# First chunk of a two-layer kernel: its first two row tiles one at a time instead of as a pair, and twelve identity matmuls at the start instead of eight

## The chip, the cores and the metric

The kernel runs on one core of one Trainium2 chip. The metric is the device time of one execution in microseconds (us), and the time of a kernel is the median of its runs. Five engines work side by side, each with its own instruction queue: PE (TensorE, matrix multiplication and transposes), DVE (VectorE), ACT (ScalarE), POOL (GpSimd) and SP (SyncE, which here only issues DMAs). They meet at semaphores. Every tensor is float32.

## The reference, cut to what matters

The whole is two layers on x of shape (16, 256, 256), that is 4096 rows of 256. Each layer is a LayerNorm, a mixer, a gate and a residual sum. The change sits at the very start of layer 0:

```python
x = L0_attn_x                                   # (16, 256, 256)
xn = _layernorm(x, axis=-1)
s = _L0_attn_ref(xn, ...)                       # diagonal recurrence over 256 steps
h = gelu(einsum('lne,he->lnh', xn, proj1) + proj1_bias)     # 256 -> 1024
g = _silu(einsum('lnh,eh->lne', h, proj2) + proj2_bias)     # 1024 -> 256
x = x + s * g
...                                             # layer 1: attention of 16 heads, a routed low-rank gate
return x
```

## The kernel before, in words

The 4096 rows are cut into 8 chunks (`NCH`) of 512 rows (`CH`). A chunk lies in SBUF as 4 row tiles (`TPC`) of 128 rows, rows on the partitions. For the projection the rows have to be turned, so that the 256 features lie on the partitions: `xnT` holds two feature halves (c = 0, 1) of 128 partitions with 512 columns, one column for each row of the chunk.

Layer 0 goes over the chunks one after the other, layer 1 after it over the same chunks in units of four heads. The first chunk of layer 0 has a function of its own, `start()`, in which nothing is ready yet: the rows, the weights and the identity matrix all have to arrive or be made first. Its helpers are:

- `warm()`: `NWARM` matmuls of the 128x128 identity with itself into a PSUM tile that nobody reads. Each shows as two records in the profile, as every float32 matmul here does.
- `stats(js)`: for each row tile j, bn_stats and bn_aggr on DVE. After an odd tile, DVE adds epsilon to the variances of the two last tiles (`ve`), and POOL raises them to the power of minus one half (`rs`).
- `apply(js)`: DVE subtracts the mean and multiplies by `rs`, which gives `xn`.
- `turn(js)`: PE transposes the two feature halves of each named tile into one PSUM tile `tp`. `keep(js, ps)`: DVE copies that to `xnT` in SBUF.
- `hide(js, f0, f1)`: for blocks fc of 128 hidden features, two matmuls (c = 0, 1) of a block of `p1T` with the columns of `xnT` of the named tiles, into a PSUM tile `ph`; then ACT computes Gelu into `hT[fc]`. There are 8 blocks (`NFC`).

`warm`, `tp` and `ph` tiles come from one ring of four PSUM banks (`ps_mm`, names r1, r2, r3, x), so that a new tile waits until the reader of the tile four places before is done.

Order: PE, DVE, ACT and POOL are wrapped in `InOrder`, which keeps the instructions of each engine in the order in which the code writes them. In between stands `later`, a list of small DVE operations (with a few on ACT and POOL) that make the recurrence's parameters; `later.write(n)` writes the next n of them into the queues, and `later.write("exp")` those up to a mark. They are needed much later, but whoever is behind them on DVE waits for them.

The loads are issued on the queues of SP and ACT at the very start: the four row tiles of chunk 0 one by one on SP, the first two quarters of `p1T` (blocks fc 0 to 1, and 2 to 3) on ACT's queue, then on SP the other half of `p1T`, chunk 1, `p2T` and the rest. None of these waits for a compute engine.

After `start()` come the second projection of chunk 0 (`pf`), the projection of chunk 1, and so on.

Of the kernel before, what the change touches and what calls it, by code (L numbers as in the profile page):

```python
# [11 lines left out]
F32 = mybir.dt.float32  # L12
# [6 lines left out]
P = 128  # L19
# [14 lines left out]
RMS_EPS = 1.1920928955078125e-07  # L34
LORA_SCALE = 32.0 / 16.0
BIG = 1e30
NWARM = 8
MAGIC = 12582912.0


# [1 line left out]
def tile_two_layers(ctx: ExitStack, tc: tile.TileContext, d: dict, out: bass.AP):  # L42
# [386 lines left out]
    with ExitStack() as l0:  # L429
# [22 lines left out]
        ps_mm = Ring("r1", "r2", "r3", "x")  # L452
# [40 lines left out]
        def norm0(ch, between=None):  # L493
            xn = a2.tile([P, TPC, D], F32, tag="xn", name=f"xn0_{ch}")
            layer_norm(sm, X[ch], xn, f"0_{ch}", v0, g0, between)
            return xn

        def turn0(ch, xn):
            xnT = a2.tile([P, 2, CH], F32, tag="xnT", name=f"xnT0_{ch}")
            if ch == 1:  # L500
                transpose_rows(ps_mm, "mm", xn, xnT, f"0_{ch}", a0, v0)
            else:
                transpose_rows(ps_mm, "mm", xn, xnT, f"0_{ch}")
            return xnT


        v0 = ve
        later = Later()
# [27 lines left out]
        def tiny(name, n=1):  # L536
            return w0.tile([P, n], F32, tag=name, name=name)
# [44 lines left out]
        f = tiny("f")  # L582
# [24 lines left out]
        for k in range(8):  # L607
            n = 1 << k
# [485 lines left out]
        def start():  # L1094

            xn = a2.tile([P, TPC, D], F32, tag="xn", name="xn0_0")
            xnT = a2.tile([P, 2, CH], F32, tag="xnT", name="xnT0_0")
            st = sm.tile([P, TPC, 6], F32, tag="ln_st", name="st_0_0")
            mv = sm.tile([P, TPC, 2], F32, tag="ln_mv", name="mv_0_0")
            ve = sm.tile([P, TPC], F32, tag="ln_ve", name="ve_0_0")  # L1100
            rs = sm.tile([P, TPC], F32, tag="ln_rs", name="rs_0_0")
            hT = [hpool.tile([P, CH], F32, tag="hT", name=f"hT_0_{fc}") for fc in range(NFC)]
            X0 = X[0]

            def warm():

                ps = ps_mm.tile([P, CH], F32, tag="mm", name="warm")
                for z in range(NWARM):
                    pe.matmul(ps[:, 0:P], ident, ident, start=True, stop=True)

            def stats(js):
                for j in js:
                    v0.bn_stats(st[:, j, :], X0[:, j, :])
                    v0.bn_aggr(mv[:, j, :], st[:, j, :])
                if js[-1] % 2:
                    z = slice(js[-1] - 1, js[-1] + 1)
                    v0.tensor_scalar(ve[:, z], mv[:, z, 1], LN_EPS, None, ALU.add)
                    g0.tensor_tensor(rs[:, z], ve[:, z], mhalf[:, z], ALU.pow)

            def apply(js):  # L1120
                for j in js:
                    v0.tensor_scalar(
                        xn[:, j, :], X0[:, j, :], mv[:, j, 0:1], rs[:, j : j + 1],
                        ALU.subtract, ALU.mult,
                    )

            def turn(js):
                ps = ps_mm.tile([P, 2, 2 * P], F32, tag="mm", name=f"tp_0_0_{js[0]}")
                for c in range(2):
                    for j2, j in enumerate(js):  # L1130
                        pe.transpose(
                            ps[:, c, j2 * P : (j2 + 1) * P], xn[:, j, c * P : (c + 1) * P], ident
                        )
                return ps

            def keep(js, ps):
                v0.tensor_copy(xnT[:, :, js[0] * P : (js[1] + 1) * P], ps)

            def hide(js, f0, f1):
                z = slice(js[0] * P, (js[1] + 1) * P)  # L1140
                for fc in range(f0, f1):
                    ph = ps_mm.tile([P, 2 * P], F32, tag="mm", name=f"ph_0_{fc}_{js[0]}")
                    for c in range(2):
                        pe.matmul(
                            ph, p1T[:, c, fc * P : (fc + 1) * P], xnT[:, c, z],
                            start=(c == 0), stop=(c == 1),
                        )
                    a0.activation(hT[fc][:, z], ph, AF.Gelu, bias=b1[:, fc : fc + 1])

            warm()  # L1150
            stats((0, 1))
            later.write(4)
            apply((0, 1))
            ps = turn((0, 1))
            stats((2,))
            keep((0, 1), ps)
            stats((3,))
            later.write(3)
            apply((2, 3))
            hide((0, 1), 0, 4)  # L1160
            ps = turn((2, 3))
            later.write("exp")
            keep((2, 3), ps)
            hide((0, 1), 4, NFC)
            hide((2, 3), 0, NFC)
            xn2 = norm0(1, lambda: later.write("angle"))
            later.write("gain")
            xnT2 = turn0(1, xn2)
            later.write()
            return xn, xnT, hT, xn2, xnT2  # L1170

        xn, xnT, hT, xn2, xnT2 = start()
        spread_rope(wraw, g0)

# [18 lines left out]
        xnT = turn0(2, xn3)  # L1193
# [13 lines left out]
        xnT = turn0(3, xn)  # L1207
# [10 lines left out]
        for ch in range(FIRST, NCH - 1):  # L1218
            xn, xnT, norm2, o = middle(ch, xn, xnT, norm2, fill, o)
# [383 lines left out]
    for i in range(LAST):  # L1603
# [4 lines left out]
        n = (i + 3) // 2 if odd else (i + 2) // 2  # L1608
        n = n if n < len(groups) else None
# [69 lines left out]
        if last is not None:  # L1679
            j = FINISH.index(r)  # L1680
# [96 lines left out]
```

## Time and profile before

| what | value |
|---|---|
| time, median of 3 runs | 930.92 us (929.54, 931.18, 930.92) |
| profiled execution, its own time | 930.62 us |
| profiled execution, span from first to last instruction | 928.7 us |
| mean granted TensorE clock over the span | 0.995 |
| PE busy | 908.6 us, 98% of the span |
| DVE, ACT, POOL busy | 71%, 49%, 60% |

A span is shorter than the time of its execution, here by 1.9 us, which lie outside the program's own instructions. "PEclk" or "granted clock" is the share of full speed that the chip's throttle gave TensorE in a stretch. A busy PE is not a PE at its peak, since matmuls overlap and their ends are modelled; the spacing of matmuls of one shape is the better measure of speed. A chain of waits is the list of what released what, followed back from the last instruction.

### The profile page before, as it was taken

What the parts mean: (1) busy time and instruction counts of PE and PEld (TensorE: products, weight loads), DVE (VectorE), ACT (ScalarE), POOL (GpSimd) and SP (SyncE); (2) the same over time, 40 slices, a digit from 0 to 9 for tenths busy, and PEclk for the clock granted to TensorE, in tenths of its full rate; (3) what the DMA queues carried; (4) which work ended last, traced back from release to release, by engine and by line L of the source; (5) the groups of instructions that cost most, each with busy time, mean ns of one, the idle gap of its engine ahead of it and who ended that gap; (6) DMA issues with size and microseconds to landing.
All of it is one profiled execution on the core that took longest, in us unless ns stands there. A gap on an engine that the chain in (4) does not pass through costs nothing.

```text
span 928.7 us, 17185 instructions
## 1 busy us (share of the span) xinstructions
PE 908.6 (98%) x5354; PEld 690.1 (74%) x5354; DVE 659.5 (71%) x2005; ACT 456.7 (49%) x1507; POOL 560.3 (60%) x875
## 2 busy tenths in 40 slices
PE   8999999999999899999999999999999999999988
PEld 7765889887757567777777777777767777777766
DVE  6883667665687688668867866886886688687652
ACT  3333255554346456645644564564556456446440
POOL 1329166778354447686586667658666764865550
PEclk9999999999999999999999999999999999999999
DMA  9730000000014777777776777777677767767860
GB/s 276 231 114 1 1 1 1 1 1 1 1 27 108 190 208 190 200 184 186 179 210 163 208 209 171 187 173 222 164 202 190 181 183 178 218 162 196 231 199 25
DMA packets 196409, 133.97 MB, mean 144 GB/s; under 512 B 142112, under 2 KB 186976, under 8 KB 196320
## 3 DMA queue, kind: packets, MB, share of 16 engines
q1 hardware_dynamic: 194192, 128.68, 52.8%
q0 software_dynamic: 1152, 3.67, 1.2%
q8 instruction: 43, 0.70, 0.3%
q10 hardware_dynamic: 976, 0.53, 0.2%
q14 instruction: 46, 0.38, 0.1%
HBM read 63.11 MB, written 52.95 MB: 125 GB/s over the span
## 4 chain that ended last, share of the span: by engine, by line
PE 89%; DVE 4%; DMA 4%; SPq 2%; POOL 1%; issue 0%; ACT 0%; POOLq 0%; ACTq 0%; DVEq 0%
PE pq L53 22%; PE sc L53 14%; PE po L53 10%; PE av L53 9%; PE ph L53 6%; PE pf L53 6%; PE r L53 5%; PE f L53 4%; PE pg L53 4%; SPq L53 2%; PE pm L53 1%; PE pkv L53 1%; PE tp L53 1%; DMA far<-turned 1%; DMA pT<-far 1%; DMA qg<-qrot 1%
## 5 line engine op out<-in xcount | busy, mean ns | idle before, releaser
L53 POOL TENSOR_SCALAR pr<-pr,sr 128x256 f32<-128x256 f32 (+7 forms) x512 | 193.3, 398 | 191.3 <-DVE sr L53 189.3
L53 ACT ACTIVATE pr<-sc,nm 128x256 f32<-128x256 f32 (+7 forms) x512 | 190.2, 382 | 238.2 <-DVE sr L53 151.6
L53 PEld LDWEIGHTS sc<-kT,qg 128*128 128x128 f32 x1024 | 157.5, 191 | 63.4 <-issue 39.9
L53 PE MATMUL sc<-kT,qg 128*128 128x256 f32 (+7 forms) x1024 | 176.5, 306 | 6.6 <-DMA qg<-qrot 2.9
L53 DVE TENSOR_REDUCE nm<-sc 128x1 f32<-128x256 f32 (+7 forms) x512 | 127.6, 301 | 6.6
L53 DVE STREAM_TRANSPOSE turned<-pr 128x512 f32<-128x512 f32 x186 | 123.2, 687 | 9.4 <-POOL pr L53 9.2
L53 PE MATMUL pq<-xnT,wlat 128*128 128x512 f32 x256 | 123.7, 606 | 0.0
L53 PE MATMUL pq<-xnT,wrope 128*128 128x512 f32 x256 | 120.2, 593 | 0.0
L53 ACT ACTIVATION_READ_ACCUMULATOR pr<-sc,nm 128x1 f32 x512 | 104.2, 203 | 0.0
L53 DVE TENSOR_TENSOR sc<-sc,kmask 128x96 f32<-128x96 f32 (+1 forms) x192 | 45.6, 238 | 66.7 <-PE sc L53 65.6
L53 PE MATMUL av<-pT,row 128*64 128x256 f32 (+1 forms) x1024 | 90.7, 329 | 0.6 <-DMA pT<-far 0.5
L53 POOL TENSOR_TENSOR qrot<-qmul,qmul 128x512 f32<-128x512 f32 x64 | 83.0, 1319 | 7.4 <-DVE qmul L53 3.4
L53 PEld LDWEIGHTS av<-pT,row 128*64 128x64 f32 x1024 | 64.4, 137 | 23.3 <-issue 0.9
L53 DVE TENSOR_TENSOR qmul<-pq,rot_q 128x512 f32<-128x512 f32 x128 | 80.8, 673 | 0.4 <-PE pq L53 0.4
L53 ACT ACTIVATE qg<-pq 64x512 f32<-64x512 f32 x128 | 75.5, 590 | 5.3 <-PE pq L53 4.5
L53 PEld LDWEIGHTS pq<-xnT,wlat 128*128 128x128 f32 x256 | 46.3, 193 | 32.3 <-issue 32.1
L53 PEld LDWEIGHTS pq<-xnT,wrope 128*128 128x128 f32 x256 | 45.7, 191 | 32.4 <-issue 32.1
L53 PEld LDWEIGHTS po<-wout,attT 128*128 128x128 f32 x416 | 58.5, 191 | 9.4 <-issue 5.0
L53 PE MATMUL po<-wout,attT 128*128 128x128 f32 (+1 forms) x416 | 64.0, 308 | 0.0
L53 PE MATMUL ph<-xnT,p1T 128*128 128x512 f32 (+1 forms) x160 | 58.1, 519 | 0.8 <-DVE xnT L53 0.8
L53 PE MATMUL pf<-p2T,hT 128*128 128x256 f32 x256 | 56.8, 379 | 0.0
L53 PEld LDWEIGHTS pf<-p2T,hT 128*128 128x128 f32 x256 | 48.2, 190 | 7.2 <-issue 0.9
(235 smaller groups left out, 1411.3 us busy)
## 6 DMA issues: line engine op xcount, KB each, us to landing
far<-turned SPq DMA_DIRECT2D x248, 192.0 KB, 4.6
pT<-far SPq DMA_DIRECT2D x62, 768.0 KB, 5.0
qg<-qrot SPq DMA_DIRECT2D x256, 64.0 KB, 2.4
x<-in_x_dram SPq DMA_DIRECT2D x7, 512.0 KB, 9.4
out_dram<-x POOLq DMA_DIRECT2D x12, 256.0 KB, 5.0
wqn_wo<-in_wq_nopeT_dram SPq DMA_DIRECT2D x4, 512.0 KB, 4.5
wqn_wo<-in_Wo_dram SPq DMA_DIRECT2D x4, 512.0 KB, 5.2
p2T<-in_proj2T_dram SPq DMA_DIRECT2D x2, 512.0 KB, 7.0
```

The costliest lines, as they stand in the source:

```text
L53: r = getattr(self.engine, name)(*args, **kw)
```

## The change

The first two row tiles go one by one through norm, transposes, copy and projection, where before they went as a pair. The number of warming matmuls goes from 8 to 12. `rs` of tile 0 and of tile 1 are now computed by a POOL instruction each (128x1), of tiles 2 and 3 still by one (128x2). For fc 0 to 3 the projection of tiles 0 and 1 is done with 128 columns at a time instead of 256, so with twice as many matmuls and Gelus, half as wide each; fc 4 to 7, and everything on tiles 2 and 3, keep their 256 columns. The statistics of tiles 2 and 3, and the first seven `later` operations, stand behind the work on tiles 0 and 1 in DVE's order; before, four of the seven stood ahead of `apply((0, 1))`, and three between the statistics and `apply((2, 3))`. The DMAs, their order and their queues stay the same.

```diff
-NWARM = 8
+NWARM = 12
...
-            def stats(js):
-                for j in js:
-                    v0.bn_stats(st[:, j, :], X0[:, j, :])
-                    v0.bn_aggr(mv[:, j, :], st[:, j, :])
-                if js[-1] % 2:
-                    z = slice(js[-1] - 1, js[-1] + 1)
+            def stats(j, n):
+
+                v0.bn_stats(st[:, j, :], X0[:, j, :])
+                v0.bn_aggr(mv[:, j, :], st[:, j, :])
+                if n:
+                    z = slice(j + 1 - n, j + 1)
                     v0.tensor_scalar(ve[:, z], mv[:, z, 1], LN_EPS, None, ALU.add)
                     g0.tensor_tensor(rs[:, z], ve[:, z], mhalf[:, z], ALU.pow)
...
-                ps = ps_mm.tile([P, 2, 2 * P], F32, tag="mm", name=f"tp_0_0_{js[0]}")
+                ps = ps_mm.tile([P, 2, len(js) * P], F32, tag="mm", name=f"tp_0_0_{js[0]}")
...
-                v0.tensor_copy(xnT[:, :, js[0] * P : (js[1] + 1) * P], ps)
+                v0.tensor_copy(xnT[:, :, js[0] * P : (js[-1] + 1) * P], ps)
...
-                z = slice(js[0] * P, (js[1] + 1) * P)
+                z = slice(js[0] * P, (js[-1] + 1) * P)
...
-                    ph = ps_mm.tile([P, 2 * P], F32, tag="mm", name=f"ph_0_{fc}_{js[0]}")
+                    ph = ps_mm.tile([P, len(js) * P], F32, tag="mm", name=f"ph_0_{fc}_{js[0]}")
...
             warm()
-            stats((0, 1))
-            later.write(4)
-            apply((0, 1))
-            ps = turn((0, 1))
-            stats((2,))
-            keep((0, 1), ps)
-            stats((3,))
-            later.write(3)
+            stats(0, 1)
+            stats(1, 1)
+            apply((0,))
+            ps = turn((0,))
+            keep((0,), ps)
+            apply((1,))
+            hide((0,), 0, 2)
+            ps = turn((1,))
+            keep((1,), ps)
+            hide((0,), 2, 4)
+            stats(2, 0)
+            stats(3, 2)
+            later.write(7)
             apply((2, 3))
-            hide((0, 1), 0, 4)
+            hide((1,), 0, 4)
             ps = turn((2, 3))
             later.write("exp")
             keep((2, 3), ps)
             hide((0, 1), 4, NFC)
             hide((2, 3), 0, NFC)
```

## The prediction, made before the changed kernel was run

> **What bounds the kernel now.** I read the page first. PE is busy for 98% of the span and carries 89% of the chain that ended last, so only time in which PE idles or runs slowly can be won.
>
> ```profile
> span 928.7 us, 17185 instructions
> ...
> PE 908.6 (98%) x5354; PEld 690.1 (74%) x5354; DVE 659.5 (71%) x2005; ACT 456.7 (49%) x1507; POOL 560.3 (60%) x875
> ...
> PE 89%; DVE 4%; DMA 4%; SPq 2%; POOL 1%; issue 0%; ACT 0%; POOLq 0%; ACTq 0%; DVEq 0%
> ```
>
> Next the waits of PE over the whole span, longest first. The second and the third wait shown lie in the stage of the change.
>
> ```profile
> PE sc L53 <- DMA qg<-qrot: 2.9, 1, 2.9
> PE tp L53 <- DVE xn L53: 2.1, 1, 2.1
> ...
> PE ph L53 <- DVE xnT L53: 0.8, 1, 0.8
> ```
>
> Then the chain in order of time (start, length, what). From 7.34 to beyond 39 us it is PE work end to end, except for the copy at 8.25: whatever makes the transposes of 14.13 end earlier moves all that follows.
>
> ```profile
> 6.88 0.42 DVE xn L53
> 7.30 0.04 issue
> 7.34 0.88 PE tp L53 x4
> 8.23 0.02 issue
> 8.25 0.70 DVE xnT L53
> 8.95 0.04 issue
> 9.00 5.13 PE ph L53 x16
> 14.13 0.44 PE tp L53 x4
> 14.56 10.36 PE ph L53 x48
> 24.93 0.87 PE tp L53 x8
> 25.80 13.82 PE pf L53 x64
> ```
>
> The first sixteen ph records take 321 ns each, the next forty-eight 216 ns at the same shape. The busy time by stretches says why (window, PE busy, granted clock, DMA share, GB/s):
>
> ```profile
> 5.30:9.00 3.70, 0.87 (x5) 0.93 0.85 240
> 9.00:11.85 2.85, 2.85 (x7) 0.50 0.96 295
> 11.85:14.00 2.15, 2.15 (x12) 0.99 1.10 349
> ...
> 305.40:308.80 3.40, 0.46 (x2) 1.00 0.92 106
> 308.80:312.20 3.40, 3.40 (x7) 0.51 0.74 270
> ```
>
> In steps of 0.1 us the clock halves at 8.47 and is full again at 11.89, 3.41 us later. The 3.41 us ahead of the fall held about 1.1 us of PE work (0.23 of warming from 5.06, 0.87 of transposes, 32%); those ahead of the rise 2.9 us (85%). After the 2.9 us wait at 305.68 it halves again, over another 3.4 us. PE's wait of 1.9 us for POOL's pr at 893 brings no fall (1.9 of 3.41 us idle is 45% busy), so I put the limit between 32% and 45%. Before 5.06 the column shows 1.00, but the warming matmuls stand (3.75 - 0.42)/15 = 222 ns apart, against (0.60 - 0.27)/3 = 109 ns for four transposes of that size at 13.96: they ran at half speed.
>
> **The change, step by step.** Times are in the profiled execution.
>
> *Warming.* 24 records for 16. The first 16 end at 5.23 as now; the other eight, at 109 ns if the clock has risen at 5.06, end at 6.1, at 222 ns they end at 7.0. I take 6.1, as the transposes at 7.34 ran at the full rate.
>
> *Tile 0.* Its statistics end at 4.67 (landing-bound, as now), ve at 4.87 (0.17 and a gap). POOL follows 0.15 later, as now (5.97 to 6.12); its one-column operation is nearest to gsq (128x1, 0.55; the two-column rs took 0.72): done at 5.57. DVE is then busy with tile 1 until ve at 5.97, whose landing (5.12) does not move. The four small operations between are gone. xn of tile 0 runs 5.9 to 6.31 (0.41 each), its two transposes 6.35 to 6.8. The copy of half the columns costs between 0.35 (half of 0.69) and 0.69; I take 0.42, near xn's 0.41 for as many elements: 7.24. Projection starts at 7.29, where now it starts at 9.00.
>
> *Narrow matmuls.* 32 records of 128 columns for 16 of 256. One costs no less than 109 ns (transposes) and hardly more than 121 ns (psq, 16 in 1.93 us, 64 columns, so the weight load's floor): 0.118 x 32 = 3.8 us for 3.45 us at 216 ns, +0.3 us of PE work. fc 0 and 1 of tile 0 end at 8.25; the transposes of tile 1 (xn ready at 7.6) follow without a wait and are copied by 9.15, under fc 2 and 3 of tile 0, which end at 9.4; tile 1's four blocks end at 11.3. Gelu: four of 0.47 become eight of between 0.24 and 0.47, paced by PE's 0.47 per block; ACT idled 4.5 us before the first. The table load is done at 6.61.
>
> *DVE behind it.* Statistics of tile 2 now wait for the second copy, though their rows land before 6: 9.1 to 9.7, tile 3 to 10.2, ve to 10.4, POOL to 11.3 (0.15 + 0.72). Seven small operations at 0.19 each end at 11.6 and are 0.3 us of delay. xn of tiles 2 and 3 ends at 12.0 and 12.4 (11.3 now). So PE, done at 11.3, idles 0.75 us: the new wait. The four transposes start at 12.05 and end at 12.9, where now they end at 14.56. Behind the transposes queue fc 4 to 7 of tiles 0 and 1, which need no more of DVE until ph 7 takes the bank of these transposes: eleven small operations (2.66 us from the start of xn, now 10.58 to 13.24) and the copy (0.69) end at 14.9, ph 7 would start at 15.5: 0.6 us of cover. Chunk 1's statistics follow, 0.4 us earlier than now, and its xn is done by 19.6; PE wants it at 22.9.
>
> *Clock.* The period 5.06 to 8.47 then holds 1.0 (warming) + 0.45 + 1.2 = 2.65 us of work, 78%, the next one 84%: no fall. Of the 1.66 us, 1.4 is the half-speed stretch (2.85 us at 0.50) that is gone. Starting 1.7 us earlier is nearly all paid back: 0.3 for narrow matmuls, 0.75 of new idling, 0.2 for tile 1's transposes, which now stand in between, and 0.2 of seams.
>
> The sum: 14.56 - 12.9 = 1.66, taken as 1.65 us. The chain is PE's without a gap from there to 276 us, and the loads wait only for each other, and land well before use (chunk 1's rows are issued at 5.78 and take 5.7 us, to 11.5; they are used at 14.8). So 930.62 - 1.65 = 929.0 us. That execution lies 0.3 us under the median of the runs. Bounds of the unknown costs: the two copies at 0.69 and the narrow records at 121 ns give 1.0 us; the copies at 0.35, POOL's one column hidden, 109 ns give 2.1 us. The forecast's own range is 928.4 to 929.7.
>
> [...]
>
> **Rivals.**
>
> *The stretch at 308.85 goes too.* The periods seen are 3.41 us long with ends at 305.43 and 308.85; the wait now fills 305.68 to 308.62. Moved 1.65 us earlier it straddles the end at 305.43, with 1.4 us of idling in one period and 1.55 us in the other, 55 to 59% busy, so no fall; that saves half of 3.4, 1.7 us: 927.3. It holds for moves from about 1.2 to 2.2 us. Against it: the phase may differ between runs, and DMA waits follow soon (3.48 us at 319.70) that can swallow it.
>
> *The phase.* If the period's ends lie elsewhere in an execution, the half-speed stretch of before differs. With ends at about 9.5 instead of 11.9, its cost is 0.3 and not 1.4 us, and the gain is 0.4 to 0.7: 930.1. The runs shown differ by 1.6 us, about one such stretch. [...]
>
> *The gain is swallowed later.* At 276 and 305 us PE waits on other engines, in chains with DMA; were their times fixed, 930.6. Against it: the chain behind the wait at 305.68 leads back over POOL, ACT and DVE to PE's own scores, which move along.
>
> *Slower: the rise comes late.* If no period is full enough until one ends at 15.3, all PE work of the stage runs at half speed: warming to 7.0, tile 0's transposes and copy to 8.0, eight records of 222 ns to 9.8, tile 1's transposes, eight more to 11.9, sixteen to 15.4, four transposes to 16.0: 1.45 us later than now, 932.1; with one more half-speed stretch after the wait of 1.5 us at 344, 933.8. It decides if the gaps of 0.3 and 0.5 us around the first copy count as idle. Against it: 85% was enough at 11.89.
>
> **How the numbers follow.** Forecast 42%, stretch at 308.85 gone as well 25%, phase 14%, swallowed 7%, slower 12%. The predicted time is the forecast's, 929.0. A difference of 0.2% (1.9 us) is about what a measurement of this kernel can tell from none; the bound below is 929.06. Of the forecast 23 points lie under it and 19 above; the stretch that goes is all under; phase and swallowed are within; of the slower case 7 points lie over 932.8, 5 within. That makes 48% faster, 45% within, 7% slower. The range 927.0 to 931.3 holds all but the slower case and the far ends of the second.
>
> **What would show it.** Right: clock 1.00 through 8.5 to 11.9, ph records of tile 0 from 7.3 some 118 ns apart, a PE wait of about 0.75 us for DVE's xn near 11.3, and the transposes of tiles 2 and 3 ended near 12.9. Wrong in part: a clock of 0.50 anywhere from 6 to 15 us; narrow records much over 121 ns; tile 0's copy later than 7.4; ph 7 waiting for the copy of tiles 2 and 3; or PE waits past 276 us that grow by what the start gave.

## The result and the profile after

| | before | changed |
|---|---|---|
| median of 21 runs each | 930.41 us (928.36 to 932.36) | 928.26 us (924.62 to 930.88) |
| ratio of the times | 1 | 0.9975, 95% interval 0.9965 to 0.9985 |
| profiled execution: time, span | 930.62, 928.7 us | 926.95, 925.2 us |
| transposes of tiles 2 and 3 end, in that execution | 14.56 us | 13.17 us |

The changed kernel is faster by 2.1 us between the medians; the ratio says 2.3 us, with 1.4 to 3.3 us as its interval. The range of the prediction holds the median, and the forecast of 1.65 us lies inside the interval. Of all the runs below one, of the mended order with eight warming matmuls, took 1902.67 us for a reason that is not known; its ratio leaves that run out, and without it the median of that version is 926.54 us and not 926.72.

From the page of the changed kernel, and of the waits of PE those that the change touches:

```profile
PE 907.9 (98%) x5378; PEld 691.2 (75%) x5378; DVE 659.8 (71%) x2007; ACT 456.8 (49%) x1511; POOL 559.3 (60%) x876
```

```profile
PE tp L53 <- DVE xn L53: 0.8, 1, 0.8
...
PE ph L53 <- DVE xnT L53: 0.5, 1, 0.5
```

PE's busy time is nearly the same (0.7 us less, with 24 records more). What shrank is the waiting at the start: 2.1 us for xn became 0.8 us, and 0.8 us for xnT became 0.5 us. The 0.8 us is not what is left of the old wait, but the new one ahead of tiles 2 and 3, as the chain shows (start, length, what):

```profile
1.48 5.32 PE warm L53 x24
6.80 0.23 PE tp L53 x2
7.06 0.44 DVE xnT L53
7.54 1.16 PE ph L53 x8
8.70 0.23 PE tp L53 x2
8.95 0.42 DVE xnT L53
...
11.92 0.34 DVE xn L53
12.39 0.78 PE tp L53 x4
13.17 10.36 PE ph L53 x48
```

From 1.48 to 8.95 the chain is almost all PE, warming included. At 8.95 it passes to DVE: copy, statistics of tiles 2 and 3, small operations, xn. PE finished tile 1's blocks at about 11.6 and started again at 12.39. Behind 13.17 everything is the old chain, 1.39 us earlier.

The clock, by periods of 3.41 us, the length of its half-speed stretch here (window, PE busy, granted clock, DMA share, GB/s):

```profile
3.08:6.50 3.42, 3.42 (x18) 1.00 0.91 284
6.50:9.91 3.41, 2.89 (x26) 1.00 0.89 280
9.91:13.32 3.41, 2.61 (x22) 1.00 1.07 341
303.46:306.87 3.41, 0.80 (x2) 1.00 0.62 96
306.87:310.28 3.41, 2.85 (x6) 0.50 0.96 223
```

The clock rose at 6.50, behind the first 3.41 us that PE's work filled, and the next two periods were 85% and 77% busy: no fall in the whole stage. (The 1.00 of the first row is not measured: the clock's record of this execution begins with that rise, and until then the warming matmuls ran at half speed: the first sixteen records stand 224 ns apart, against 109 ns at the full clock.) After the long wait at 304 the period was 23% busy, and the next 3.4 us ran at half speed, as before the change.

From the start to 302 us the changed execution stays 1.4 us ahead. The other 2 us between the two spans come from layer 1, by the starts of DVE's transposes: 0.7 us between 327 and 349, 0.35 us given back by 652, 1.35 us between 652 and 724, where the profiled execution of before had waited 1.11 us for a pT transfer at 688 and the changed one had no such wait, and 0.3 us by 792. Further profiled executions of the kernel before differ from its first one by 0.2 to 1.4 us between 652 and 750, so I take these for draws and not for the change; no run separates the two.

### The profile page after: what moved, and what is told of

It reads as the page before. It is cut to its first block, busy times and chain, and to the rows that moved or that the text cites. A ratio compares the mean times of both kernels' runs of the same rounds, so it can differ in the third digit from the quotient of the medians.

```text
span 925.2 us, 17242 instructions
## 1 busy us (share of the span) xinstructions
PE 907.9 (98%) x5378; PEld 691.2 (75%) x5378; DVE 659.8 (71%) x2007; ACT 456.8 (49%) x1511; POOL 559.3 (60%) x876
## 4 chain that ended last, share of the span: by engine, by line
PE 90%; DVE 5%; POOL 2%; DMA 1%; ACT 1%; SPq 1%; issue 1%; ACTq 0%; DVEq 0%; POOLq 0%
PE pq L53 22%; PE sc L53 14%; PE po L53 10%; PE av L53 9%; PE pf L53 6%; PE ph L53 6%; PE r L53 5%; PE pg L53 5%; PE f L53 4%; PE pm L53 1%; PE pkv L53 1%; PE tp L53 1%; POOL pr L53 1%; DMA qg<-qrot 1%; DVE nm L53 1%; PE pb L53 1%
## 5 line engine op out<-in xcount | busy, mean ns | idle before, releaser
L53 PE MATMUL ph<-xnT,p1T 128*128 128x512 f32 (+2 forms) x176 | 56.9, 478 | 0.5 <-DVE xnT L53 0.5
```

The lines of the kernel that those rows point to most:

```text
L53: r = getattr(self.engine, name)(*args, **kw)
```

## The experiments

Four questions: which part of the change removes the half-speed stretch, what the new wait costs, what either part does without the other, and how the kernel before varies.

**The split alone, with eight warming matmuls.**

```diff
-NWARM = 12
+NWARM = 8
```

> The row tiles one by one, but eight warming matmuls as before. Clock theory (the half-speed stretch that went is what counts, and the four further warming matmuls are what removes it): the warming ends at 5.2 us, PE idles for about 1 us before tile 0's transposes, and in a part of the executions a period still falls under the limit; gain 0.8 to 1.6 us, ratio to before 0.9983 to 0.9991. Split theory (the earlier start of the projection in single row tiles is the gain): the whole of it, ratio 0.9970 to 0.9980, and a profile whose first transposes start earlier than the 6.6 us of the changed kernel.

Measured: 927.79 us (12 runs), ratio 0.9978 (0.9966 to 0.9989). That is the whole gain, as the split theory had it. The clock rose at 5.58 in its profile, and the following period shows why it stayed:

```profile
5.58:8.99 3.41, 2.65 (x21) 1.00 0.87 260
```

With tile 0 alone the transposes start at 5.82 and the projection at 6.78. So this period is 78% busy, where the same kind of period of the kernel before (5.06 to 8.47) was 30% busy and the clock fell behind it. In this form the split gains little by its early start as such: the transposes of tiles 2 and 3 end at 12.41, within 0.3 us of the two profiles of the warming alone below (12.68 and 12.55), in which nothing starts earlier. It fills the gap that cost the clock. Nor do the four further warming matmuls add to it in these profiles: with twelve the warming holds tile 0's transposes back from 5.82 to 6.80, and the stage ends 0.8 us later than here (0.5 us in the second execution, below). The medians don't tell eight from twelve (927.79 here, 928.26 and 928.05 for the change).

**The warming alone.** The kernel before with twelve warming matmuls.

```diff
-NWARM = 8
+NWARM = 12
```

> The kernel before with twelve warming matmuls and nothing else changed. Clock theory: PE is busy to about 6.8 us and again from 7.3, no period falls under the limit, the sixteen first ph records run at 216 ns, the transposes of tiles 2 and 3 end near 13.0 us where they ended at 14.56; gain 1.3 to 2.3 us, ratio 0.9975 to 0.9986, nearly that of the whole change. Split theory: no gain, ratio 0.9995 to 1.0005, since nothing starts earlier.

Measured: 927.07 us (6 runs), ratio 0.9962 (0.9949 to 0.9976); the interval is wide, so it was run again (below). The chain of this kernel:

```profile
1.48 5.49 PE warm L53 x24
6.97 0.78 PE tp L53 x4
...
7.77 0.70 DVE xnT L53
...
8.52 3.72 PE ph L53 x16
12.24 0.44 PE tp L53 x4
```

The sixteen ph records take 3.72 us for 5.13, the full rate, and the transposes of tiles 2 and 3 end at 12.68, half a microsecond ahead of the whole change: here DVE did the statistics of tiles 2 and 3 in the shade of PE's work, and PE has no wait for xn of these tiles.

**Two warming matmuls.** The kernel before with `NWARM = 2`.

> The kernel before with two warming matmuls in place of eight. If the eight seldom carried a full clock as far as the projection, taking six away costs little: 0.1 to 0.6 us, ratio 1.0001 to 1.0006, with the first projection at half speed to about 12 us or later. If the eight did hold the clock in most executions and the profiled one was an exception, it costs 1.0 to 1.6 us, ratio 1.0011 to 1.0017.

Measured: 932.50 us (12 runs), ratio 1.0018 (1.0001 to 1.0035). The point lies just above the upper expectation (1.0011 to 1.0017), and the interval leaves both open. In the profile the clock rose only at 14.53, the ph records took 6.50 us and the transposes of tiles 2 and 3 ended at 15.80. The period ahead of the one that brought the rise:

```profile
7.70:11.11 3.41, 2.63 (x7) 1.00 0.97 293
```

77% busy was not enough (the clock column shows 1.00 here only because its record begins with the first rise; the sixteen ph records stand 6.50/16 = 406 ns apart where at full rate they stand 216 ns apart, which says half speed).

**DVE's order mended.** The changed kernel, with the statistics of tiles 2 and 3 where DVE waits for PE, and the seven small operations behind `apply((2, 3))`.

```diff
             ps = turn((0,))
+            stats(2, 0)
             keep((0,), ps)
...
             ps = turn((1,))
+            stats(3, 2)
             keep((1,), ps)
             hide((0,), 2, 4)
-            stats(2, 0)
-            stats(3, 2)
-            later.write(7)
             apply((2, 3))
+            later.write(7)
```

> The changed kernel with DVE's order mended: the statistics of tile 2 stand ahead of the first copy and those of tile 3 ahead of the second, where DVE waits for PE anyway, and the seven small operations stand behind apply of tiles 2 and 3. If PE's wait of 0.8 us for xn of tiles 2 and 3 is real time on the path: the transposes of tiles 2 and 3 end near 12.2 us in place of 13.2, and the gain over before grows by 0.7 to 1.2 us to a ratio of 0.9963 to 0.9970. If that time is swallowed by later waits: ratio 0.9970 to 0.9980 as for the changed kernel.

Measured: 926.68 us (12 runs), ratio 0.9962 (0.9949 to 0.9975). The instructions of PE and DVE in order of time:

```profile
8.26 2.84 PE L53 MATMUL ph<-xnT,p1T 128*128 128x128 f32 x24
...
8.95 0.74 DVE L53 TENSOR_SCALAR xn<-x,mv,rs 128x256 f32<-128x256 f32 x2
...
10.94 0.60 PE L53 MATMUL tp<-ident,xn 128*128 128x128 f32 x4
```

xn of tiles 2 and 3 is done by 9.7, and PE goes from ph to the transposes without a wait. They end at 11.54, 1.6 us ahead of the changed kernel; of these, 0.5 us is the earlier end of the warming (6.31 for 6.80), as the clock rose a microsecond earlier (5.46 for 6.50). The other 1.1 us are the wait of 0.80 us and 0.34 us in the transposes themselves, four of which take 0.44 us in a row with ph and 0.78 us behind the wait. So the new wait costs 1.1 us and not only the 0.8 us that the view of the waits shows, and the stage ends earlier than the 12.2 that I expected; the ratio lies just past the expected 0.9963 to 0.9970. The median is 1.4 to 1.6 us under the changed kernel's. The interval shows that this version beats the kernel before. That it beats the changed one is not shown by the ratios, whose intervals overlap; it rests on the stage's end and on the like median of the mended order with eight warming matmuls, below.

**The split with two warming matmuls.** The changed kernel with `NWARM = 2`.

> The changed kernel with two warming matmuls in place of twelve. If the row tiles one by one gain by keeping PE at work ahead of the projection, so that the clock rises earlier and stays, they gain without warming too: the clock rises near 10 us where the kernel before with two warming matmuls rose at 14.5, and the time is 1.0 to 2.5 us under that kernel's (932.5 us median), ratio to before 0.9980 to 0.9997. If the gain of the split hangs on the warming, the time is that of the kernel with two warming matmuls, ratio 1.0010 to 1.0030.

Measured: 930.22 us (12 runs), ratio 1.0000 (0.9987 to 1.0014), 2.3 us under the unsplit kernel with two by the medians of two sets of runs, and 1.7 us by the ratio of each to the kernel before in its own set. The clock rose at 11.85, where 10 was expected, and the transposes of tiles 2 and 3 ended at 13.79, where unsplit they ended at 15.80. So the split gains without warming too, but the ratio lies just above what was expected (0.9980 to 0.9997), and eight or twelve warming matmuls are worth another 2 us.

**The mended order with eight warming matmuls.**

> The kernel with the mended DVE order and eight warming matmuls in place of twelve. If with single row tiles the four further warming matmuls are not needed (the split alone held the clock in the profile with eight), the time stays at that of twelve, ratio 0.9955 to 0.9975, and the first transposes start about 0.5 us earlier. If they are needed, a half-speed stretch shows up between 6 and 12 us and the ratio goes to 0.9975 to 0.9990.

Measured: 926.72 us (12 runs), ratio 0.9970 (0.9954 to 0.9986): within the first expectation, and the same median as with twelve. The transposes of tiles 2 and 3 ended at 11.30. The clock rose at 5.77, and no half-speed stretch shows in the stage behind it.

**The change and the warming alone, side by side.**

> The changed kernel once more, to stand beside the next one on the same chip: ratio 0.9970 to 0.9982. If the split adds to the warming, it is 0.5 us or more faster than the kernel with the warming alone; if PE's new wait for xn of tiles 2 and 3 takes back what the earlier start gives, the two are within 0.7 us of each other or this one is slower.

> The kernel before with twelve warming matmuls once more, for more runs than the first six: ratio 0.9965 to 0.9985, if the twelve hold the clock in every execution; above 0.9990 if the first six runs were lucky draws.

Measured: 928.05 us (12 runs) for both, with ratios 0.9978 (0.9964 to 0.9992) for the change and 0.9979 (0.9965 to 0.9993) for the warming alone. On top of the warming, the split in the form of this change adds nothing that these runs can measure. The transposes of tiles 2 and 3 ended at 12.92 (change) and 12.55 (warming): as in the first pair, the warming alone ends the stage 0.4 to 0.5 us earlier. The ratio of the warming alone lies in its first expectation. That its first six runs were 1 us lower, at 927.07 us, may be a draw; the two intervals overlap.

**The kernel before, in four more profiled executions.**

> The kernel before, looked at again. If the clock's periods lie elsewhere in every execution, the first projection's sixteen records take anything from 4.4 to 6.5 us, and in some executions the clock rises only near 13 to 14.5 us, so that the transposes of tiles 2 and 3 end at 14.0 to 15.5 us (14.56 in the first look), later on average than the first look showed. If the phase is fixed, all four looks end within 0.2 us of 14.5 with the clock full at 11.9.

> The second of four looks at the kernel before: free periods, transposes of tiles 2 and 3 ended anywhere from 14.0 to 15.5 us; fixed phase, 14.5 with the clock full at 11.9.

> The third of four looks at the kernel before: free periods, transposes of tiles 2 and 3 ended anywhere from 14.0 to 15.5 us; fixed phase, 14.5 with the clock full at 11.9.

> The fourth of four looks at the kernel before: free periods, transposes of tiles 2 and 3 ended anywhere from 14.0 to 15.5 us; fixed phase, 14.5 with the clock full at 11.9.

Measured: transposes of tiles 2 and 3 ended at 14.26, 15.36, 14.29 and 14.29, the times were 929.46, 930.43, 928.79 and 932.50 us. Three of them resemble the one shown first, with the clock full again at 11.8 to 12.0, and sixteen ph records of 5.32 to 5.41 us for 5.13. The second is of another kind; its chain, and its periods:

```profile
8.75 6.18 PE ph L53 x16
14.93 0.44 PE tp L53 x4
```

```profile
3.52:6.94 3.42, 1.95 (x10) 1.00 0.93 265
6.94:10.35 3.41, 2.63 (x8) 1.00 0.95 291
```

The eight warming matmuls lay across two periods and filled neither, the next one was 77% busy, and the clock rose at 13.76. So the phase is not fixed, though in four executions of five the periods' ends stood within 0.2 us of each other, which neither expectation foresaw.

## Why the prediction was right, and where it was not

- *The clock carries the gain.* Predicted 1.4 of 1.66 us from the half-speed stretch that goes, with the rest paid back. The warming alone, which starts nothing earlier, gives the same ratio as the whole change side by side (0.9979, 0.9965 to 0.9993, and 0.9978, 0.9964 to 0.9992). This holds.
- *The four further warming matmuls remove the stretch.* They do, but the split does so alone as well (0.9978, 0.9966 to 0.9989). The two parts are substitutes: each keeps PE busy ahead of the projection (78% of 5.58 to 8.99 with the split alone; all of 3.45 to 6.86 and 77% of 6.86 to 10.27 with the warming alone), and once one does the other has nothing to remove. The step on the clock counted warming and narrow records together (2.65 us, 78%) and did not ask what either gives alone; the expectation that followed from it for the split alone (0.9983 to 0.9991) missed by its median for that reason.
- *Warming ends at 6.1.* It ended at 6.80, 6.55 in the second profiled execution, since the clock rose at 6.50 and 5.96 and not at 5.06. The bound of 7.0 held it. Tile 0's transposes then waited for the warming and not for xn, which had been ready at 5.7. The prediction had xn of tile 0 at 6.31, since it held the landing of tile 1's rows at 5.12; DVE began on them at 4.52 and 4.58 in the two executions of the change, and at 4.52 to 4.66 in the four further ones of the kernel before, so the first execution was the exception. The projection started at 7.54 and 7.29 for a predicted 7.29; since it came by another path, that the second hits the forecast is luck.
- *Copy of half the columns 0.42, narrow records 118 ns.* Measured 0.42 us, and (2.84 - 0.27)/23 = 112 ns. The 121 ns of psq were thus no floor of the weight load: these records load weights of the same 128x128, 24 of them in 2.76 us.
- *The new wait of 0.75 us, 0.3 us of it for the seven operations.* Measured 0.80 us; rs was done at 11.50 and xn began at 11.83. That it is time on the path is shown by the mended order, which gains 1.1 us of the stage without it.
- *The sum.* The stage was to end at 12.9 and ended at 13.17 and 12.92. But 1.65 us was the gain against one execution of the kernel before. Over five of them its stage ends at 14.26 to 15.36, 14.55 on average, against 13.05 in the two of the change: 1.5 us. The medians differ by 2.1 us. Of the remaining 0.6 us I can't say whether it is a draw; the ratio's interval (1.4 to 3.3 us) holds both. The clock's term was sized on one execution too: the sixteen first ph records took 5.13 us there, 5.47 us on average over the five, and 3.72 us at the full clock, so the stretch costs about 1.75 us and not 1.4.
- *Rival: the stretch at 308.85 goes.* A half-speed stretch began at 306.87 in the first profiled execution of the change and at 306.33 in the second (mean granted clock from 300 to 320 us 0.91 in both). The step that failed was to carry the period ends of one execution over to another. One execution without the stretch (the warming alone, second time; 1.00 from 300 to 320 us) shows that it can happen, in the way that the rival named: there the wait straddles a period's end at 305.58, with 43% and 51% of the two periods busy.
- *Rival: the phase.* Right that the ends can lie elsewhere (the clock rose at 11.89 in the first execution of the kernel before and at 13.76 in the second of the four above), wrong in its effect: I let it shrink the loss of before, and it also makes it larger (15.36).
- *Rival: the rise comes late.* It exists, and these profiles show it in the kernel before and not in the change: 77% busy was too little at 10.35 in the second of the four executions above and at 11.11 with two warming matmuls. With twelve warming matmuls, one whole period fell into the warming in each of the five profiles taken.
- *Rival: swallowed later.* Not so: at 302 us the change is still 1.4 us ahead.

In the five profiles with twelve warming matmuls the warming starts at 1.48 us each time, but the clock rose at 5.21, 5.46, 5.96, 6.50 or 6.86 us. So the ends of the periods lie elsewhere from one execution to the next, which one trace could not show. Behind its first rise and until the tail of the execution, the clock stayed full or half for multiples of 3.41 us: full for 88 (6.50 to 306.87), half for one and full for 180 (310.29 to 924.69) in the first profile of the changed kernel, and full for 87 (11.89 to 308.85), half for one and full for 180 in that of the kernel before.

## What to carry to other kernels

Where a kernel's start has short bursts of matmuls between waits, count PE's busy share over stretches as long as those in which the clock changed, 3.41 us in these traces. Two changes that filled the same stretch were worth one of them (ratios 0.9978 and 0.9979 alone, 0.9978 together), so try each alone; and when work is split to start earlier, look at what the other engine's fixed order now does last, since here that took back about 1.1 us of the stage, which moving three calls gave again.

## What the runs showed of the hardware that was not expected

- The clock rose and fell at different busy shares of the 3.41 us ahead. At half speed it stayed low after 57% and 77% (3.52 to 6.94 and 6.94 to 10.35 in the second of the four further executions of the kernel before), after 63% (5.03 to 8.44 in the split with two warming matmuls) and after 77% (7.70 to 11.11 in the unsplit kernel with two). It rose after 84% (306.87 to 310.28 in the changed kernel) and 85% (8.47 to 11.89 in the first execution of the kernel before, 2.35 to 5.76 in the mended order with eight). At full speed it fell after 14% and 30% (305.43 to 308.84 and 5.06 to 8.47 in the first execution of the kernel before), 23% (303.46 to 306.87 in the changed kernel) and 36% (883.19 to 886.60 in its second execution). It did not fall after 61% (5.21 to 8.62 in the warming alone, second time), nor in the first executions of the two kernels after any period of 62% or more.
- Between 43% and 57% it did either. The clock stayed full after 45% (892.5 to 895.9 in the first execution of the kernel before), after 57% (342.98 to 346.39 in the same, 341.01 to 344.42 in the changed kernel) and after 43%, in the warming alone the second time (first view below). It fell after 44% (340.47 to 343.88 in the second execution of the change) and after 57%, in the first of the four further executions of the kernel before (second view). So the prediction's limit between 32% and 45% does not hold. What decides there stays open; the ends of matmuls, and with them PE's busy time, are modelled.

```profile
302.17:305.58 3.41, 1.48 (x4) 1.00 0.65 100
305.58:308.99 3.41, 1.74 (x6) 1.00 0.87 146
```

```profile
889.02:892.43 3.41, 1.95 (x16) 1.00 0.47 110
892.43:895.85 3.42, 3.03 (x13) 0.50 0.94 327
```

- Such stretches go with a good part of the spread of the times. Among the 21 runs of the changed kernel the three with a mean clock of 0.994 took 930.11 to 930.88 us, the five with 1.000 took 924.62 to 928.26 us. A mean clock lower by 0.006 over 928 us means 5.6 us lost, about three stretches of 3.4 us at half speed with 1.7 us lost in each; the profiled execution with 0.994, the second of the change, has three, at 306.33, 343.88 and 886.60. Which waits draw one differs from run to run: the first profile of the change has one ahead of its tail, at 306.87. The five runs with 1.000 still differ by 3.6 us, so the clock is not all of it.
